# Layer 2 of a four-layer network: rows of B asked for earlier, tokens' transposes in the results' PSUM bank, expert-bias products moved into the send steps

## The chip, the core and the metric

The kernel runs on one core of one Trainium2 chip. The metric is the time of one execution on the device, in microseconds (us). Engines are named as in the profile: PE is TensorE, DVE is VectorE, ACT is ScalarE, POOL is GpSimd, and SP is SyncE, which issues most DMAs. Each engine works through its own instructions in the order in which they were issued and waits on semaphores for the others.

## The reference

The network has four layers on 16 sequences of 256 tokens with 128 features. Each layer normalises `x`, computes an attention-like part `s` and a feed-forward part `f` from the same normalised tokens, and adds `s * silu(f)` to `x`. The change lies in layer 2, whose two parts are these (shortened):

```python
# s: a selective scan (d_inner 256, 16 states per channel)
xi, z = split(layernorm(xn) @ W_in); xc = silu(conv4(xi) + conv_b)
dt_lo, B, C = split(xc @ W_xp, [8, 24]);  delta = softplus(dt_lo @ W_dt + dt_bias)
for t: h = h * exp(delta[t] * A) + (delta[t] * xc[t]) * B[t];  y[t] = (h * C[t]).sum(state)
s = ((y + xc * D_skip) * silu(z)) @ W_out + xn
# f: 16 experts (128 -> 512 -> 128), the two most likely of each token
p = softmax(xn @ Wr + br); gate = p at the two largest, 0 elsewhere
f = sum_e gate[:, e] * (relu(xn @ W1[e] + b1[e]) @ W2[e] + b2[e])
```

The part `gate @ b2` of `f` doesn't depend on the experts' results. It is computed by itself, as eight products of 128x512, and is what the text calls the bias products.

## The kernel before

All tokens stand in SBUF as 32 tiles of 128 tokens. `layer2` runs the scan of `attn2` and the experts of `ffn2` beside one another, in one long loop of steps written out in Python.

**The scan.** The 4096 tokens are eight groups of 512 (two sequences). A group takes 32 steps, so there are 256. Every even step handles two of the 16 states for one half of the 256 channels, for 512 tokens at once. DVE multiplies the input by the rows of B (`dbb`, L1113) and runs the scan (`st`, L1117). The product with the rows of C (`hc`, L1130) is made by POOL one pair of steps later, beside the next scan, or by DVE itself while POOL is sending tokens (steps below 32) and gathering them (from the step `fetch` on). ACT computes the decays (`dab`, L1103) four steps ahead. PE adds the products up over the states by multiplying with the identity (`sums`, L1140), five steps behind. There are two buffers for scans, three for `hc` and three for decays. `prepare` computes the inputs of the next group in small parts that are hung on steps; its products share the two PSUM banks `psa` (tile `pa`).

**Rows of B and C.** `broadcast(n)` asks SP for two rows of B and two rows of C from DRAM, each laid over 128 partitions (512 KB, L94). Both were asked for three steps ahead of their first use, and each kind has two buffers, so that a request waits until the last reader of its buffer is through.

**The experts.** The routing part of `ffn2` finds each token's two experts and its places in a DRAM buffer of 47 blocks of 256 rows (one expert for each block). Then:

- `send`: in steps 0 to 31 POOL writes the tokens to their places by 64 indirect DMAs, two per step (L1333).
- `begin`, in step 33, loads the tokens of the first blocks (L1345) and weights (L1354, L1356), and transposes two blocks.
- From step 34 on a `piece` per step, four to a block: PE multiplies by W1 (`hidden`, L1377, twice per block, into the bank `psh`), ACT applies bias and relu (`relu`, L1391), and PE multiplies the block before by W2 (`result`, L1402, two halves, into the bank `psy`). Beside the second half PE transposes the tokens of a later block (`turn`, L1365, into the bank `psh` too). One step later `evict` copies the result (L1414) and writes it to DRAM from SP (`store`, L1415), copies the transposed tokens (`turned`, L1370), and asks SP for the weights two blocks on and the tokens three blocks on.
- Two steps of every 32 hold no piece, so that `evict` falls on steps 2, 6, 10... of a cycle of four in one half of the time and on steps 0, 4, 8... in the other.
- `bring` and `weigh`, from step 239 on: POOL gathers each tile's two result rows (L1451, six buffers per kind) and DVE adds them to `f`, weighted (L1461); after every fourth tile come the gated addition and the normalisation for layer 3, whose `rstd` (L158, L159) is POOL's.

The routing ended with the bias products: PE multiplied (L1319) into the one PSUM buffer `tot`, ACT copied (L1320), eight times, before the buffer could be used again. The tile framework sets the order between this part and the first steps; within the loop of steps `pin` keeps each engine to the order in which the code was written.

```python
            for k in range(max(at) + 1):
                if k < SENT:
                    for i in range(2):
                        experts["send"](2 * k + i)
                scan["step"](k, k < SENT or k >= fetch)
                for f_ in at.get(k, ()):
                    f_()
```

Of the kernel before, what the change touches and what calls it, by code (L numbers as in the profile page):

```python
# [10 lines left out]
F32 = mybir.dt.float32  # L11
# [8 lines left out]
P = 128  # L20
# [53 lines left out]
class Net:  # L74
# [734 lines left out]
    def layer2(self, ydram, consts):  # L809
# [10 lines left out]
        with ExitStack() as ctx:  # L820
# [21 lines left out]


            k = SENT + 1
            later(k, experts["begin"])
# [75 lines left out]
    def attn2(self, ctx, psa, consts, later):  # L921
# [34 lines left out]
        def prepare(gr, base):  # L956
# [108 lines left out]

            def broadcast(n):
                for i, name in ((8, "bn"), (24, "cn")):
                    d[name, n] = self.load(
                        bc, d["dr"][i + n : i + n + 2, :].partition_broadcast(P), name, shape=[P, 2, T]
                    )  # L1070

# [9 lines left out]
            parts += [(25, delta), (26, inputs)]  # L1081
            parts += [(29 + 2 * n, call(broadcast, n)) for n in range(0, N, 2)]
            parts.sort(key=lambda p: p[0])
# [120 lines left out]
    def ffn2(self, ctx, consts, f):  # L1204
# [12 lines left out]
        gate = cp.tile([P, K, NT], F32, name="gate")  # L1217
        bank = cp.tile([P, NB], I32, name="bank")
        b1s = cp.tile([P, 4, NB], F32, name="b1s")
        with tc.tile_pool(name="f2_r", bufs=1, **side) as rp, tc.tile_pool(  # L1220
# [83 lines left out]
            for i in range(4):  # L1304
                nc.tensor.transpose(
                    pg[:, i, :], e[:, 8 * i : 8 * i + 8, :].rearrange("p t e -> p (t e)"), self.ident
                )
            gT = rp.tile([P, 4, P], F32, name="gT")
            nc.scalar.copy(gT, pg)


            b2 = rp.tile([P, 8, D], F32, name="b2")
            nc.gpsimd.memset(b2, 0.0)  # L1313
            for j in range(8):
                nc.sync.dma_start(b2[E * j : E * j + E, j, :], a["L2_ffn_b2"])
            for c in range(NT // 4):
                pf = ps.tile([P, 4, P], F32, name="tot")
                o = 4 * (c % 2)
                nc.tensor.matmul(pf, gT[:, c // 2, :], b2[:, o : o + 4, :], start=True, stop=True)  # L1319
                nc.scalar.copy(f[:, 4 * c : 4 * c + 4, :], pf)  # L1320

# [3 lines left out]
        rp = enter("f2_x", 3)  # L1325
        gp = enter("f2_g", 6)
        psh = enter("f2_ph", 1, space=PSUM)
        psy = enter("f2_py", 1, space=PSUM)
        placed, got = [], {}

        def send(i):
# [29 lines left out]
        def turn(j):  # L1361
            if j < NB:
                got[j]["px"] = px = psh.tile([P, R], F32, name="ph")
                for q in range(2):
                    nc.tensor.transpose(px[:, q * P : (q + 1) * P], got[j]["xr"][:, q, :], self.ident)  # L1365

        def turned(j):
            if j < NB:
                got[j]["xT"] = rp.tile([P, R], F32, name="xT")
                nc.scalar.copy(got[j]["xT"], got[j]["px"])  # L1370

# [23 lines left out]
        def result(j, q):  # L1395
            if j < 0:
                return
            if q == 0:
                got[j]["py"] = psy.tile([P, 2, D], F32, name="py")
            py, h, w2 = (got[j][n] for n in ("py", "h", "w2"))  # L1400
            for c in range(4):
                nc.tensor.matmul(  # L1402
                    py[:, q, :],
                    h[:, c, q * P : (q + 1) * P],
                    w2[:, c, :],
                    start=(c == 0),
                    stop=(c == 3),
                )

        def store(j):  # L1410
            if j < 0:
                return
            y = pool.tile([P, 2, D], F32, name="y")
            nc.scalar.copy(y, got.pop(j)["py"])  # L1414
            nc.sync.dma_start(ys[j * R : (j + 1) * R, :].rearrange("(q p) d -> p q d", p=P), y)  # L1415
# [43 lines left out]
        def weigh(t):  # L1459
# [7 lines left out]
            "send": send, "begin": begin, "piece": piece, "pieces": 4 * NB + 4, "bring": bring,  # L1467
            "weigh": weigh,
        }
# [494 lines left out]
```

## Time and profile before

| | us |
|---|---|
| median of three runs (lowest, highest) | 3040.19 (3035.48, 3047.49) |
| the profiled execution, its own time | 3071.67 |
| its span | 3069.7 |
| layer 2 from the first scan to the last (in the profile) | 875.2 to 1615.6 |

The page gives, for the whole span, PE as busy for 2502.2 us, DVE for 1997.0, ACT for 1479.0 and POOL for 1345.6. These are averages over very different stages; layer 2's loop of steps takes a quarter of the span, and what bounds it changes along the way. The lines of a timeline give start and duration in us, engine, line, operation, tiles and shape; in brackets stands the idle time of the engine before it and what ended that.

### The profile page before, as it was taken

The numbers are of one execution on the slowest core, as the hardware profiler recorded it, in microseconds if no ns is written. First come the engines' busy times: TensorE is split into PE (matmuls) and PEld (weight loads), VectorE is DVE, ScalarE is ACT, GpSimd is POOL, SyncE is SP. The second block draws the span as 40 slices with busy tenths as digits, with TensorE's granted clock in tenths as the row PEclk, the third lists the DMA queues.
The fourth block names the chain that finished last, engine by engine and source line by source line (L and its number), as shares of the span: only waits on it lengthen the run. The fifth ranks groups of instructions, "written<-read, shape, count | busy, mean of one in ns | idle before, by whom it ended". The sixth has DMA issues, their size and how long they took to land. (4 is left out here: it accounts for less than half of the span.)

```text
span 3069.7 us, 47743 instructions
## 1 busy us (share of the span) xinstructions
PE 2502.2 (82%) x17560; PEld 1605.9 (52%) x17575; DVE 1997.0 (65%) x4037; ACT 1479.0 (48%) x3291; POOL 1345.6 (44%) x1156
## 2 busy tenths in 40 slices
PE   5999893779654799999934688898999987899987
PEld 4666582556421455555513455554566654566654
DVE  5666433335573978787885467787778745788845
ACT  2555461223332566667621345443677641577743
POOL 2000002123327255555566788875455522455531
PEclk8999895879756799999966589898899989899988
DMA  2111002000112456555521211011000000000000
GB/s 66 29 29 29 4 2 98 1 18 14 39 55 85 139 174 195 169 185 183 176 94 41 46 25 39 22 37 51 13 13 14 15 1 2 14 15 15 13 3 28
DMA packets 136214, 168.24 MB, mean 55 GB/s; under 512 B 20658, under 2 KB 100413, under 8 KB 135981
## 3 DMA queue, kind: packets, MB, share of 16 engines
q1 hardware_dynamic: 127404, 147.09, 16.1%
q0 software_dynamic: 6496, 17.05, 1.6%
q8 instruction: 139, 2.28, 0.3%
q10 hardware_dynamic: 2080, 1.05, 0.1%
q14 instruction: 95, 0.77, 0.1%
HBM read 126.96 MB, written 29.79 MB: 51 GB/s over the span
## 5 line engine op out<-in xcount | busy, mean ns | idle before, releaser
L335 DVE TENSOR_REDUCE nmax<-pa 128x2 f32<-128x512 f32 x512 | 330.5, 684 | 151.2 <-PE pb L326 124.9
L316 PE MATMUL pa<-kT,qT 32*128 32x256 f32 x2048 | 388.0, 430 | 21.5 <-DMA kT<-qkd 10.8
L326 PE MATMUL pb<-qa,kT 32*128 32x256 f32 x2048 | 382.9, 418 | 6.9 <-ACT e L340 6.8
L340 ACT ACTIVATE e<-pb 128x512 f32<-128x512 f32 x512 | 280.2, 595 | 207.0 <-PE pb L326 204.9
L1130 POOL TENSOR_TENSOR hc<-st,cn 128x1024 f32<-128x1024 f32 x104 | 245.7, 2362 | 248.4 <-DVE dbb L1113 193.0
L316 PEld LDWEIGHTS pa<-kT,qT 32*128 32x128 f32 x2048 | 253.0, 199 | 120.9 <-issue 50.8
L1117 DVE TENSOR_TENSOR_SCAN st<-dab,dbb 128x1024 f32<-128x1024 f32 x128 | 292.7, 2287 | 25.3 <-POOL hc L1130 6.9
L1140 PE MATMUL py<-hc,ident 128*128 128x512 f32 x512 | 284.1, 653 | 23.6 <-POOL hc L1130 11.7
L326 PEld LDWEIGHTS pb<-qa,kT 32*128 32x128 f32 x2048 | 250.2, 193 | 20.5 <-ACT e L340 14.5
L343 POOL TENSOR_TENSOR e<-e,pen 128x512 f32<-128x512 f32 x176 | 234.3, 1356 | 42.1 <-ACT e L340 42.0
L1776 ACT ACTIVATE p<-ps,nm,rl 128x128 f32<-128x128 f32 x512 | 227.2, 464 | 42.3 <-DVE nm L1769 42.0
L1785 POOL TENSOR_TENSOR p<-p,den 128x512 f32<-128x512 f32 x128 | 132.8, 1038 | 246.1 <-DVE den L1784 224.8
L1103 ACT ACTIVATE dab<-dl,A_log 128x512 f32<-128x512 f32 x256 | 178.7, 717 | 115.9 <-DVE st L1117 73.8
L1687 PE MATMUL pm<-wqkv,hT 128*128 128x512 f32 x384 | 207.4, 654 | 17.8 <-DVE hT L1681 8.7
L1113 DVE TENSOR_TENSOR dbb<-du,bn 128x1024 f32<-128x1024 f32 x128 | 179.3, 1401 | 43.2 <-DMA bn<-dr 41.4
L1710 POOL TENSOR_TENSOR rot<-rot,sn 128x512 f32<-128x512 f32 x128 | 162.3, 1268 | 99.4 <-DVE sn L1705 83.1
L1140 PEld LDWEIGHTS py<-hc,ident 128*128 128x128 f32 x512 | 98.8, 209 | 114.8 <-issue 74.9
L1313 POOL MEMSET b<- 128x1024 f32 x1 | 1.0, 951 | 327.0 <-PE pm L367 327.0
L367 PE MATMUL pm<-e,vaug 128*32 128x256 f32 x2048 | 140.7, 420 | 0.5 <-POOL e L343 0.5
L1757 PE MATMUL ps<-kT,qT 64*64 64x128 f32 x2048 | 139.9, 289 | 0.0
L1757 PEld LDWEIGHTS ps<-kT,qT 64*64 64x64 f32 x2048 | 93.7, 137 | 82.0 <-issue 80.1
L1700 ACT ACTIVATE sq<-pm 128x512 f32<-128x512 f32 x128 | 74.9, 615 | 118.3 <-PE pm L1687 112.6
(372 smaller groups left out, 5556.5 us busy)
## 6 DMA issues: line engine op xcount, KB each, us to landing
bn<-dr SPq DMA_DIRECT2D x64, 512.0 KB
cn<-dr SPq DMA_DIRECT2D x64, 512.0 KB
w<-in_L_ffn_W_dram SPq DMA_DIRECT2D x94, 256.0 KB
qkd<-qk SPq DMA_DIRECT2D x32, 256.0 KB
v<-v SPq DMA_DIRECT2D x64, 128.0 KB
f_y<-y SPq DMA_DIRECT2D x47, 128.0 KB
f_x<-zero POOLq DMA_DIRECT2D x8, 704.0 KB
xr<-f_x SPq DMA_DIRECT2D x44, 128.0 KB
```

The lines of the kernel that those rows point to most:

```text
L316: nc.tensor.matmul(pa[:, t, :], qbuf[b % 4][r : r + 32, g, ts], kbuf[b % 4][r : r + 32, g, :], start=True, stop=True,)
L326: nc.tensor.matmul(pb[:, t, :], kbuf[b % 4][r : r + 32, g, ts], qas[m // 8][r : r + 32, g % 2, :], start=True, stop=True,)
L335: nc.vector.tensor_reduce(nbuf[n // 8 % 2][:, :, u // 4, u % 4, 8], pa, AX.X, ALU.max, negate=True)
L340: nc.scalar.activation(e, pb, AF.Exp, scale=scale)
L343: eng.tensor_mul(e, e, pens[m // 16])
L1113: mul = nc.vector.tensor_mul(db, du, d["bn", n])
L1117: nc.vector.tensor_tensor_scan(wide(d["st", r]), wide(d.pop(("da", r))), wide(db), 0.0, ALU.mult, ALU.add)
L1130: ins = eng.tensor_mul(d["hc", r], d.pop(("st", r)), d["cn", r // 4 * 2])
L1140: nc.tensor.matmul(d["py", h], self.ident, d["hc", r - r % 2][:, r % 2, :], start=(n == 0), stop=(n == N - 1))
L1687: nc.tensor.matmul(pj, hTs[b % 3][:, t * P : (t + 1) * P], d["qkv"][:, j * 512 : (j + 1) * 512], start=True, stop=True,)
L1757: nc.tensor.matmul(ps[i][64 * half : 64 * half + 64, c, w, :], qT[f, 2 * u + c, q0 : q0 + 64], kT[f, 2 * u + c, keys[half] : keys[half] + ...
L1776: nc.scalar.activation(p[:, c, w, :], ps[i][:, c, w, :], AF.Exp, scale=r[:, w, 0, h + 2 * c : h + 2 * c + 1], bias=nm[:, c, w : w + 1], ac ...
```

## The change

Four things are changed.

- The rows of B are asked for two steps earlier (position 27 + 2n in place of 29 + 2n); the rows of C stay.
- `turn` writes into the second half of the bank that holds the results; that bank is now one tile `halves` for the whole time, with `halves[:, 0]` for results and `halves[:, 1]` for transposed tokens.
- The bias products leave the routing. Step 1 clears a buffer (on DVE, before on POOL) and loads `b2` into it by eight small DMAs on SP; the eight products run in steps 4, 7, 16, 19, 22, 25, 28 and 31, each into a bank of `psa`, and ACT copies each one a step later.
- The gathers' buffers go from six to four per kind. The clearing buffer takes the place of one of the two buffers `h` until step 31.

```diff
@@ layer2
+            later(1, experts["spread"])
+            for c in range(NT // 4):
+                k = (4, 7, 16, 19, 22, 25, 28, 31)[c]
+                later(k, lambda c=c: experts["biases"](psa, c))
+                later(k + 1, lambda c=c: experts["biased"](c))
             k = SENT + 1
             later(k, experts["begin"])
@@ attn2, prepare
-            def broadcast(n):
-                for i, name in ((8, "bn"), (24, "cn")):
-                    d[name, n] = self.load(
-                        bc, d["dr"][i + n : i + n + 2, :].partition_broadcast(P), name, shape=[P, 2, T]
-                    )
+            def broadcast(name, n):
+                i = {"bn": 8, "cn": 24}[name] + n
+                d[name, n] = self.load(
+                    bc, d["dr"][i : i + 2, :].partition_broadcast(P), name, shape=[P, 2, T]
+                )
...
-            parts += [(29 + 2 * n, call(broadcast, n)) for n in range(0, N, 2)]
+            for n in range(0, N, 2):
+                parts += [(27 + 2 * n, call(broadcast, "bn", n)), (29 + 2 * n, call(broadcast, "cn", n))]
@@ ffn2, routing
+        gT = cp.tile([P, 4, P], F32, name="gT")
...
-            gT = rp.tile([P, 4, P], F32, name="gT")
             nc.scalar.copy(gT, pg)
-            b2 = rp.tile([P, 8, D], F32, name="b2")
-            nc.gpsimd.memset(b2, 0.0)
-            for j in range(8):
-                nc.sync.dma_start(b2[E * j : E * j + E, j, :], a["L2_ffn_b2"])
-            for c in range(NT // 4):
-                pf = ps.tile([P, 4, P], F32, name="tot")
-                o = 4 * (c % 2)
-                nc.tensor.matmul(pf, gT[:, c // 2, :], b2[:, o : o + 4, :], start=True, stop=True)
-                nc.scalar.copy(f[:, 4 * c : 4 * c + 4, :], pf)
...
-        gp = enter("f2_g", 6)
+        gp = enter("f2_g", 4)
...
         psy = enter("f2_py", 1, space=PSUM)
+        halves = psy.tile([P, 2, 2, D], F32, name="py")
+        def spread():
+            b2 = pool.tile([P, 4, R], F32, name="h")
+            got["b2"] = b2 = b2.rearrange("p c (o d) -> p (c o) d", d=D)
+            nc.vector.memset(b2, 0.0)
+            for j in range(8):
+                nc.sync.dma_start(b2[E * j : E * j + E, j, :], a["L2_ffn_b2"])
+        def biases(ps, c):
+            got["pf"] = pf = ps.tile([P, 4, P], F32, name="pa")
+            o = 4 * (c % 2)
+            nc.tensor.matmul(pf, gT[:, c // 2, :], got["b2"][:, o : o + 4, :], start=True, stop=True)
+        def biased(c):
+            nc.scalar.copy(f[:, 4 * c : 4 * c + 4, :], got["pf"])
@@ turn, turned, result, store
-                got[j]["px"] = px = psh.tile([P, R], F32, name="ph")
                 for q in range(2):
-                    nc.tensor.transpose(px[:, q * P : (q + 1) * P], got[j]["xr"][:, q, :], self.ident)
+                    nc.tensor.transpose(halves[:, 1, q, :], got[j]["xr"][:, q, :], self.ident)
...
-                nc.scalar.copy(got[j]["xT"], got[j]["px"])
+                nc.scalar.copy(got[j]["xT"], halves[:, 1].rearrange("p q d -> p (q d)"))
...
-            if q == 0:
-                got[j]["py"] = psy.tile([P, 2, D], F32, name="py")
-            py, h, w2 = (got[j][n] for n in ("py", "h", "w2"))
+            py, h, w2 = halves[:, 0], got[j]["h"], got[j]["w2"]
...
-            nc.scalar.copy(y, got.pop(j)["py"])
+            nc.scalar.copy(y, halves[:, 0])
+            del got[j]
```

More of the change, by code (lines that the diff above doesn't have):

```diff
@@ L1467, in ffn2 @@
             "send": send, "begin": begin, "piece": piece, "pieces": 4 * NB + 4, "bring": bring,
-            "weigh": weigh,
+            "weigh": weigh, "spread": spread, "biases": biases, "biased": biased,
         }
```

## The prediction

> **What bounds the kernel now.** I read three stages of layer 2 in the timeline, then the waits and PE's groups for steps 34 to 239.
>
> *Routing to sends.* The timeline around 911 to 937 us:
>
> ```profile
> 929.45 2.07 PE L1319 MATMUL tot<-b,gT 128*128 128x512 f32 x2 [0.68 <-ACT xnT L1320]
> 931.55 0.59 ACT L1320 COPY xnT<-tot 128x512 f32<-128x512 f32 x1 [2.16 <-PE tot L1319]
> 932.19 2.08 PE L1140 MATMUL py<-hc,ident 128*128 128x512 f32 x2 [0.68 <-ACT xnT L1320]
> ...
> 936.83 1.23 DVE L1130 TENSOR_TENSOR hc<-st,cn 128x1024 f32<-128x1024 f32 x1 [25.86 <-PE py L1140]
> ```
>
> Product and copy alternate on one buffer, 2.75 us for each of eight (910.2 to 932.2). The sums stand behind them on PE, no `hc` buffer comes free, and DVE stands for 25.86 us. Later in the same timeline:
>
> ```profile
> 972.69 1.34 PE L1014 MATMUL pa<-xz,W_xp 128*40 128x512 f32 x2
> 992.75 0.96 POOL L1333 DMA_INDIRECT f_x<-xn,slot  x1 [0.30 <-issue]
> 995.52 2.25 POOL L1345 DMA_DIRECT2D xr<-f_x  x3 [1.81 <-DMA f_x<-xn,slot]
> 1000.04 0.58 ACT L1020 COPY xd<-pa 40x512 f32<-40x512 f32 x1 [19.68 <-remote]
> 1000.09 1.22 DVE L1130 TENSOR_TENSOR hc<-st,cn 128x1024 f32<-128x1024 f32 x1 [9.98 <-remote]
> ```
>
> ACT copies a product that PE had finished at 974.03 only at 1000.04: between about 945 and 1000, while POOL sends, PE's signals come late. DVE waits 8.00, 10.67, 5.74 and 9.98 us before four `hc`: 34.4 us. POOL's sends run from 911.3 at 1.26 us each whatever the others do, and the first tokens can be loaded from 995.5.
>
> *Expert pieces.* The waits from 1040 to 1548, two of PE's groups there, and two windows in which DVE stands:
>
> ```profile
> DVE dbb L1113 <- DMA bn<-dr: 41.4, 19, 7.5
> POOL hc L1130 <- PE py L1140: 39.6, 17, 5.7
> ...
> L1377 PE MATMUL ph<-xT,w 128*128 128x256 f32 x376 | 103.0, 398 | 18.4 <-ACT xT L1370 18.1
> L1365 PE MATMUL ph<-ident,xr 128*128 128x128 f32 x90 | 18.3, 285 | 18.4 <-ACT h L1391 18.3
> ...
> 1150.00:1155.00 5.00, 5.00 (x20) 2.50 (x18) 0.00 (x0) 4.94 (x5) 0.00 (x0) 1.00 0.90 231
> 1308.00:1314.00 6.00, 6.00 (x23) 2.98 (x21) 0.00 (x0) 5.94 (x6) 0.64 (x1) 1.00 0.88 250
> ```
>
> In the windows (length, then busy time and count of PE, PEld, DVE, ACT, POOL) DVE does nothing, waiting for rows of B, and PE is busy all along; so it is in every such wait that I opened. PE's idle time is 41 of these 508 us, and 36.4 of that is the bank which `turn` shares with `hidden`. PE sets the pace here; the rows are late because they stand on SP behind a `store` that waits for PE.
>
> *Gathers.*
>
> ```profile
> 1636.84 1.30 DVE L172 TENSOR_SCALAR xn<-x,ln_mv,ln_r 128x128 f32<-128x128 f32 x4 [4.40 <-POOL ln_r L159]
> 1636.99 1.13 POOL L1451 DMA_INDIRECT got<-f_y,slot  x1 [0.19 <-issue]
> 1637.87 1.38 DVE L1461 SCALAR_TENSOR_TENSOR xnT<-got,gate,xnT 128x128 f32<-128x128 f32 x4
> ```
>
> From 1612 to 1656 POOL never stands for more than 0.5 us and DVE waits for it.
>
> **The change, part by part.** The sum is made against the profiled execution, 3071.67 us, and then carried to the median, which is 31.5 us lower.
>
> *Bias products out of the routing.* Sums can follow the copy of `gT` at 910.2, so `hc` runs at about 911 in place of 936.8: 25.8 us sooner for the scan. What is late next is the tokens. Undisturbed, six pairs of steps and a `prepare` took 1002.6 to 1037.9, that is 5.1 us a pair and 4.9 extra. Before without late signals: scan of step 8 at 939.3, of step 32 at 939.3 + 12 x 5.1 + 4.9 = 1005.4. After: at 980. But `turn` in step 33 needs tokens that land at about 1000, and PE holds the sums behind it; so the first expert product starts at about 1003 in place of 1007 (1040.4 in the profile, with the 34.4 us). With late signals in both, it moves from 1040.4 to about 1017, or to 1003 if they vanish. The gain in this stage is therefore 3 to 4 us at the least and 23 to 37 at the most. Which end counts is decided by whether runs without a profile have late signals. The profiled execution is 31.5 us above the median, close to the 34.4; I take them for the profile's own and count 4 us.
>
> *Bias products in the steps.* Eight products (2 x 0.43 to 1.04 us), eight copies of 0.59 on ACT, on engines that are busy for 49 and 19 of the 100 us from 900 on. In steps 8 and 19 a `prepare` product must wait for the copy to free a bank; behind that wait on PE are sums which DVE needs a pair later. All of it ends before the tokens come: nothing, or at most 8 x 0.59 + 2 x 5.1 = 15 us if DVE, not the tokens, were last. The clearing on DVE lies before the places are known, where DVE is busy for 33 of 36 us: 1 us (POOL took 0.95 for the same shape). Eight DMAs at 0.32 to 0.42 on SP's queue in step 1 stand ahead of the rows for step 8 on: 3 us there, against rows due some 12 us later, so none.
>
> *`turn` in the results' bank.* `turn` no longer waits for `relu`, `hidden` no longer for the copy of the tokens. Not all returns. The next `hidden` needs the same `relu`, after 0.3 us of transposes and 0.86 of sums; the next `result` needs the copy `y`, which stands just ahead of `xT` on ACT. The gaps in PE's timeline: three of 3.64 us, where `hidden` and a sum (1.7) certainly fit, and after which the clock is down (`hidden` 2.08 for 1.03, sum 1.91 for 1.02, `result` 1.92 for 1.05: 2.8 us more); six of 1.68 to 3.18 on `relu`, of which 1.2 each; three of 1.28, gone. Least: 3 x 1.7 + 6 x 1.2 = 12. Most: 36.4 + 3 x 2.8 = 45. I take 3 x 4.5 + 6 x 1.2 + 3 x 1.28 = 25, since the gaps lie where ACT is late for its own reasons. A cost: `y` waits for the transposes (0.2 us), the next `result` for the copy `xT` (0.38). Between stand a sum, `hidden` and a sum, 2.6 us at full clock, which hide it.
>
> The Trainium skill ("PSUM — Partial Sum Buffer", section on bank collisions) speaks against this part: PSUM is to be guarded by whole bank, so that two halves of one bank can't be written by PE and read by ACT at once. If nothing hid that, 47 blocks by 0.6 us would take back 28 us, and the sum would end near the median of before.
>
> *Rows of B.* Where `evict` falls on steps 2, 6, 10, the order on SP stays what it was, as nothing stands between the old and the new place. Where it falls on 0, 4, 8, and at the change-over, the rows now pass one `store`, two weights and one load of tokens, and that is where the long waits are (before steps 60, 64, 80, 124, 144, 188, 208). Passed over, these wait at most for a product that DVE has made. The waits of 41.4 us go, but PE was busy through them: 0 to 41, and I count 0 on top of the 25, which DVE could not follow without it.
>
> *Four gather buffers.* `bring(t)` must now wait for `weigh(t-4)`. Laid over the trace, 13 of 32 tiles were issued up to 4.9 us ahead of that, 30.7 us together. Most lie where POOL had time in hand; in the stretch from 1612 three (tiles 22, 26, 30) come straight after POOL's `rstd`, 1.6 us each. Between 0 and 31; I take 5.
>
> Sum: 4 + 25 - 1 - 5 = 23 less. Unprofiled 3040.2 - 23 = **3017 us**; a profile would show about 20 to 30 us more off, some 3020 of its own time.
>
> **The rivals.**
>
> 1. *Late signals are real.* Then the 23 to 37 us of the first stage count, taken as 31: 3040 - 31 - 25 + 6 = 2990. For: they hold ACT and DVE alike. Against: the 31.5 us.
> 2. *The pace is DVE's.* The rows' 41.4 come whole, in place of the 25: 3040 - 4 - 41 + 6 = 3001. Against: PE full in the windows.
> 3. *The stalls only move.* PE's waits reappear at `result` and at ACT, 6 us stay: 3040 - 4 - 6 + 6 = 3036, no change. For: ACT is busy for 339 of 508 us and in order.
> 4. *Slower: the gathers.* POOL and DVE take turns. From 31 us, if each measured wait is passed on, to 8 x 7.4 = 59 if DVE's work per four tiles (2.8 weighing, 1.4 adding, 1.9 statistics, 1.3 normalising) never overlaps POOL's 10: middle 45, 3040 - 4 - 25 + 1 + 45 = 3057. It decides from 43 us on, or 31 with only 12 from PE.
>
> **How the numbers follow.** About 0.5% (15 us) is what a measurement of this kernel can tell from no change: faster ends at 3025, slower begins at 3055. Chances: forecast 0.45, rivals 0.22, 0.05, 0.15, 0.13. The forecast's own range is 3003 to 3031; a quarter of it is above 3025. Faster: 0.34 + 0.22 + 0.05, and 0.02 of the third; slower 0.13, of the fourth and the worst of the third; the same 0.24. The range 2984 to 3050 leaves out the lower third of the first rival and most of the fourth.
>
> **What would show it.** L1140 follows L1305 on PE, and DVE's 25.86 us go. L1365 has no wait for L1391, L1377 at most a few us for L1370; `dbb` waits for `bn` under 8 us; PE's idle time from the first to the last piece falls from 41 to under 20 us, and those pieces take some 483 us in place of 508. POOL shows waits for L1461 in the gathers. Wrong if the first expert product starts as late as before, if PE's waits return under L1402, or if the stretch from the first gather to the last is longer by over 10 us.

## The result, and the profile after

The changed kernel takes 3039.16 us (median of 12 runs, 3034.81 to 3052.78); the kernel before, on the same chip, 3044.29 us (12 runs). The ratio is 0.9983 with a 95% interval of 0.9964 to 1.0002: 5 us less, and by this measurement no change. Its profiled execution took 3041.83 us, with a span of 3039.9. So 27 of the 30 us between the two profiled executions are the excess of the one of before over its own median (3071.67 against 3044.29).

In the changed kernel the lines have moved: `dbb` L1119, `st` L1123, `hc` L1136, sums L1146, send L1347, tokens L1359, `turn` L1378, `turned` L1383, `hidden` L1390, `relu` L1404, `result` L1413, `y` L1425, gathers L1463, `weigh` L1473; in `prepare`, `rest` is L1053, `exact` L1061, `delta` L1064, and POOL's last writes to `dl` are L1069.

The timeline of the changed kernel from the first send on (start, duration, engine, line; in brackets the idle time before):

```profile
901.52 3.03 POOL L1347 DMA_INDIRECT f_x<-xn,slot  x1 [44.37 <-DVE slot L1279]
...
906.04 1.23 DVE L1136 TENSOR_TENSOR hc<-st,cn 128x1024 f32<-128x1024 f32 x1
...
916.90 1.22 DVE L1119 TENSOR_TENSOR dbb<-du,bn 128x1024 f32<-128x1024 f32 x1
916.99 1.96 POOL L1347 DMA_INDIRECT f_x<-xn,slot  x1 [0.30 <-issue]
```

No `hc` stands for 25.86 us any more; from there until 985 us DVE never stands for more than 0.5 us. But the send that begins at 916.99, while DVE is in `dbb`, takes 1.96 us, where most take 0.96. At the end of the sends:

```profile
985.49 2.29 DVE L1123 TENSOR_TENSOR_SCAN st<-dab,dbb 128x1024 f32<-128x1024 f32 x1
...
999.50 2.25 POOL L1359 DMA_DIRECT2D xr<-f_x  x3 [1.91 <-issue]
...
1002.11 0.69 PE L1378 MATMUL py<-ident,xr 128*128 128x128 f32 x2 [25.26 <-DMA xr<-f_x]
...
1006.30 1.90 PE L1390 MATMUL ph<-xT,w 128*128 128x256 f32 x4
...
1006.54 0.75 DVE L1152 SCALAR_TENSOR_TENSOR xz<-xz,D_skip,py 128x512 f32<-128x512 f32 x1 [18.76 <-PE py L1146]
```

The scan reaches the step that needs the tokens 20 us early, and PE and DVE stand until they land. The 25.86 us have become 25.26 on PE and 18.76 on DVE.

For the expert pieces, the waits from 1007 to 1511 (engine, tile and line, what ended the wait: total us, times, longest):

```profile
ACT dab L1109 <- POOL dl L1069: 30.5, 6, 6.1
DVE du L1053 <- ACT u L1050: 28.0, 6, 5.5
...
PE py L1413 <- ACT xT L1383: 12.3, 6, 2.8
...
PE py L1378 <- DMA xr<-f_x: 11.3, 12, 2.2
...
PE ph L1390 <- ACT h L1404: 8.7, 6, 2.4
...
DVE dbb L1119 <- DMA bn<-dr: 3.0, 6, 1.1
```

DVE's 41.4 us for rows of B are 3.0, and PE's 36.4 us between `turn` and `hidden` on the shared bank are gone. In their place DVE waits for `u` 28.0 us (17.4 before), and PE waits at `result` for the copy `xT`, at `turn` for the tokens, and at `hidden` itself for `relu`. PE's idle time from step 36 to 240 is 39.5 us (40.8 before). One of the windows in which DVE now stands, ahead of a `rest`:

```profile
1131.60:1136.80 5.20, 5.20 (x27) 3.66 (x26) 0.00 (x0) 4.97 (x9) 1.78 (x1) 1.00 0.32 96
```

It looks like those of before (DVE nothing, PE full), but the thing waited for is another. In the gathers, from 1510 to 1627:

```profile
POOL got L1463 <- DVE xnT L1473: 18.7, 12, 3.1
```

`bring` waits for `weigh`, as foreseen, and first to last gather takes 115.1 us.

### The profile page after: what moved, and what is told of

Its sections match the earlier page's. It is cut to its first block, busy times and chain, and to the rows that moved or that the text cites. A ratio compares the mean times of both kernels' runs of the same rounds, so it can differ in the third digit from the quotient of the medians.

```text
span 3039.9 us, 47776 instructions
## 1 busy us (share of the span) xinstructions
PE 2481.5 (82%) x17560; PEld 1603.5 (53%) x17575; DVE 2015.2 (66%) x4038; ACT 1475.7 (49%) x3291; POOL 1361.3 (45%) x1155
## 5 line engine op out<-in xcount | busy, mean ns | idle before, releaser
L1136 POOL TENSOR_TENSOR hc<-st,cn 128x1024 f32<-128x1024 f32 x104 | 247.0, 2375 | 203.2 <-DVE dbb L1119 105.1
L1123 DVE TENSOR_TENSOR_SCAN st<-dab,dbb 128x1024 f32<-128x1024 f32 x128 | 292.8, 2287 | 31.5 <-POOL hc L1136 11.2
L1146 PE MATMUL py<-hc,ident 128*128 128x512 f32 x512 | 277.7, 639 | 21.5 <-POOL hc L1136 13.9
L1699 PE MATMUL pm<-wqkv,hT 128*128 128x512 f32 x384 | 204.0, 644 | 18.2 <-DVE hT L1693 8.7
L158 POOL TENSOR_SCALAR ln_r<-ln_mv 128x4 f32<-128x4 f32 x32 | 7.5, 233 | 471.0 <-DVE ln_st L168 418.0
L1119 DVE TENSOR_TENSOR dbb<-du,bn 128x1024 f32<-128x1024 f32 x128 | 195.1, 1524 | 5.3 <-DMA bn<-dr 3.0
L1146 PEld LDWEIGHTS py<-hc,ident 128*128 128x128 f32 x512 | 96.8, 205 | 108.9 <-issue 83.0
L1413 PEld LDWEIGHTS py<-w,h 128*128 128x128 f32 x752 | 100.1, 195 | 60.6 <-issue 37.7
```

Of the source, the lines that this page charges most:

```text
L1119: mul = nc.vector.tensor_mul(db, du, d["bn", n])
L1123: nc.vector.tensor_tensor_scan(wide(d["st", r]), wide(d.pop(("da", r))), wide(db), 0.0, ALU.mult, ALU.add)
L1136: ins = eng.tensor_mul(d["hc", r], d.pop(("st", r)), d["cn", r // 4 * 2])
L1146: nc.tensor.matmul(d["py", h], self.ident, d["hc", r - r % 2][:, r % 2, :], start=(n == 0), stop=(n == N - 1))
L1699: nc.tensor.matmul(pj, hTs[b % 3][:, t * P : (t + 1) * P], d["qkv"][:, j * 512 : (j + 1) * 512], start=True, stop=True,)
```

## The experiments

The starts of the scan's steps mark the same points in every kernel. The table has, from each profile, the first expert product counted from the first scan, the time from the scan of step 36 to that of step 240 (the pieces), and first to last gather; and the ratio of the times to those of before, with its interval.

| run | ratio | first product | 36 to 240 | gathers |
|---|---|---|---|---|
| before | 1 | 165.2 | 500.4 | 107.9 |
| changed kernel | 0.9983 (0.9964 to 1.0002) | 130.4 | 501.2 | 115.1 |
| rows_alone | 0.9987 (0.9969 to 1.0004) | 137.3 | 501.8 | 107.1 |
| turn_alone | 0.9984 (0.9970 to 0.9998) | 134.3 | 502.4 | 106.4 |
| bias_alone | 0.9989 (0.9973 to 1.0006) | 127.9 | 502.4 | 115.0 |
| gathers4_alone | 1.0023 (1.0012 to 1.0034) | 138.6 | 505.6 | 115.4 |
| pe_light | 0.9924 (0.9895 to 0.9953) | 127.6 | 482.3 | 114.6 |
| dve_light | 0.9999 (0.9977 to 1.0022) | 130.3 | 504.2 | 114.6 |
| prep_early | 0.9964 (0.9938 to 0.9990) | 127.8 | 494.2 | 115.4 |
| turn_early | 0.9998 (0.9972 to 1.0024) | 128.3 | 502.9 | 115.1 |
| sends_one_operand | one run | 126.2 | 501.5 | 114.8 |
| pieces_one_operand | 0.9954 (0.9933 to 0.9975) | 127.4 | 490.8 | 115.0 |
| scan_further_ahead | 0.9951 (0.9934 to 0.9968) | 134.4 | 501.1 | 116.0 |
| prep_dve_gather6 | 0.9910 (0.9895 to 0.9926) | 128.4 | 481.9 | 106.3 |
| all_of_these | 0.9876 (0.9857 to 0.9894) | 131.4 | 479.9 | 109.1 |
| all_but_turn | 0.9880 (0.9857 to 0.9902) | 133.6 | 479.7 | 109.2 |
| all_but_rows | 0.9905 (0.9884 to 0.9925) | 133.4 | 485.1 | 109.2 |
| all_turn_sooner | 0.9945 (0.9908 to 0.9982) | 131.6 | 506.8 | 109.1 |
| all_pe_light | 0.9825 (0.9797 to 0.9854) | 131.6 | 461.7 | 109.1 |

Each stage is from one profile. before and gathers4_alone, whose pieces are the same, differ by 5.2 us in them, so that a difference of that size in the pieces alone is no finding.

### The parts of the change, one at a time

**rows_alone**, against the kernel before:

```diff
-            parts += [(29 + 2 * n, call(broadcast, n)) for n in range(0, N, 2)]
+                parts += [(27 + 2 * n, call(broadcast, "bn", n)), (29 + 2 * n, call(broadcast, "cn", n))]
```

> The kernel before, with rows of B asked for two half-steps sooner and nothing else changed. Theory 'stalls move': DVE's 41.4 us of waits for bn go to under 8 us, but dbb then starts earlier and meets POOL's hc and the waits of the prepare chain (du for u, dl for u) grow by as much; time within 5 us of before. Rival 'a part eats the gain of another' : rows are worth 10 us or more by themselves (faster by over 0.3%), or cost as much because tokens now land behind them.

501.8 us, and a time that can't be told from before.

**turn_alone**: `halves`, with `turn`, `turned`, `result` and `store` as in the change.

> The kernel before, with the tokens' transposes in the results' bank and nothing else changed. Theory 'stalls move': PE's 36.4 us of waits on the bank of hidden go, but come back at result (for the copies y and xT) and at the tokens, the pieces take 508 us as before; time within 5 us of before. Rival 'eaten by another part': this part alone gives the 12 to 25 us of the prediction, and one of the other parts takes it back.

502.4 us. The ratio is worth 5 us with an interval of 1 to 9, which the pieces of the profile do not show; 12 to 25 is out of the question.

**bias_alone**: `spread`, `biases` and `biased` in the send steps, `gT` kept, four gather buffers.

> The kernel before, with the bias products in the send steps, gT kept, and four gather buffers in place of six (without that it doesn't fit); rows of B and the transposes as before. Theory 'stalls move': the 25.86 us before the second hc go, sends begin 10 us sooner but each takes 1.5 us in place of 1.26 while DVE is busy, so the tokens land some 3 to 10 us later than the scan needs them and the first expert product starts 5 to 10 us sooner at most; the gathers take 7 us more; together within 6 us of before. Rival 'eaten': this part is slower than before by 7 us or more by itself, so that it hides a gain of the transposes.

The first expert product comes 127.9 us after the first scan. In rows_alone, turn_alone and gathers4_alone, whose send stage is that of before, it comes after 137.3, 134.3 and 138.6; so this part is worth some 9 us, and the gathers take most of it back.

**gathers4_alone**:

```diff
-        gp = enter("f2_g", 6)
+        gp = enter("f2_g", 4)
```

> The kernel before with four gather buffers in place of six and nothing else changed. Theory: bring waits for weigh of four tiles before; the stretch from first to last gather grows by some 7 us (107.9 to 115 us) and so does the time (+4 to +9 us). Rival: the 7 us seen there in the changed kernel come from the earlier start, and this alone costs 0 to 2 us.

7 us slower (0.0023 x 3040; interval 4 to 10), and the gathers show it. POOL's waits there:

```profile
POOL got L1451 <- DVE xnT L1461: 19.9, 15, 3.4
```

So no part hides another's large gain: "eaten" falls, and the pieces are 500 to 506 us with each part and without.

### What paces the pieces

**pe_light**, against the changed kernel:

```diff
-            for c in range(4):
+            for c in range(2):
...
-                    stop=(c == 3),
+                    stop=(c == 1),
```

> The changed kernel with half of the second expert product left out (two of four products in each result): 376 products of 0.112 us less on PE, 42 us, between steps 36 and 240, which take 501 us in every profile so far; the other engines keep their work. Theory A (PE sets the pace of the pieces, 437 us of products at the spacing of the full clock, 40 us idle and the rest a lower clock): 36 to 240 falls by 35 to 45 us. Theory B (DVE sets it: 420 us busy and some 50 us of waits in the prepare chain, in order): it falls by 0 to 8 us. Theory C (a ring: PE, ACT and DVE take turns in holding each other up): 12 to 28 us.

18.9 us of the 42 arrive, so PE sets the pace for a part of the time only. That is theory C's range, not A's.

**dve_light**:

```diff
+            if h == 1 and self.SENT + 8 <= k < self.fetch:
+                outputs(k - 2, False)
+                db = d["bn", n]
+            else:
...
```

> The changed kernel with the product of du and B left out in every second pair of the pieces (the scan reads the rows of B as they are): some 50 dbb of 1.6 us less on DVE, 75 to 80 us, and as many less that can collide with POOL's hc. Theory A (PE sets the pace): steps 36 to 240 stay at 501 us within 8. Theory B (DVE): they fall by 50 to 78 us, until PE's 460 binds, so at least 40. Theory C (a ring): 12 to 28 us.

504.2 us, but the run doesn't answer its question. DVE's groups between steps 36 and 240 (busy us, mean ns of one, then the idle time before them and what ended it):

```profile
L1127 DVE TENSOR_TENSOR_SCAN st<-dab,bn 128x1024 f32<-128x1024 f32 x50 | 130.3, 2606 | 23.0 <-ACT dab L1109 19.8 <-POOL hc L1140 0.2
L1127 DVE TENSOR_TENSOR_SCAN st<-dab,dbb 128x1024 f32<-128x1024 f32 x53 | 121.2, 2287 | 24.5 <-POOL hc L1140 18.3 <-DVE dbb L1123 0.5
L1123 DVE TENSOR_TENSOR dbb<-du,bn 128x1024 f32<-128x1024 f32 x52 | 119.2, 2291 | 5.8 <-DMA bn<-dr 5.7
```

A scan that reads `bn` from SBUF takes 2606 ns in place of 2287, and the `dbb` that are left 2291 in place of 1598: DVE's busy time fell by 18 us (421.7 to 403.6), not by 75. DVE's weight had to be asked in another way. (The expectation of all_but_rows, below, still counts these 80 us as left out; 18 were.)

**pieces_one_operand**:

```diff
+            if self.SENT <= k < self.fetch:
+                mul = nc.vector.tensor_scalar_mul(flat(db), flat(d["bn", n]), 0.5)
...
```

> The changed kernel with dbb in the steps of the pieces made from B alone (half of B in place of du times B): DVE reads one operand from SBUF there. In the changed kernel 102 of these products take 162.9 us, 1598 ns each, where one undisturbed takes 1.22; so 38 us of DVE's time go, and nothing is added elsewhere. Theory B (DVE sets the pace): steps 36 to 240, 501.2 us, fall by 25 to 38 us. Theory A or D (PE and the prepare chain set it, DVE has time in hand): 0 to 6 us, and DVE waits longer for u, dl or bn.

DVE's group of `dbb` there:

```profile
L1121 DVE TENSOR_SCALAR dbb<-bn 128x1024 f32<-128x1024 f32 x101 | 123.8, 1225 | 8.5 <-DMA bn<-dr 6.3
```

39 us of DVE's time went, and 10.4 us of the pieces: above the range of A and D, far below B's. POOL's products beside it became shorter as well (its busy time fell from 300.3 to 285.3 us), so DVE's weight isn't seen by itself. Most of what is gained lies in steps 28 to 31 of a group, as the table below and prep_dve_gather6 show.

**prep_early**:

```diff
-            parts += [(14, silu), (16, call(down, 0)), (17, call(down, 1)), (18, downed)]
-            parts += [(19, call(up, 0)), (19, call(up, 1)), (20, call(biased, 0)), (20, call(biased, 1))]
-            parts += [(21, size), (21, small), (22, plus), (23, rest), (23, log), (24, exact)]
+            parts += [(14, silu), (16, call(down, 0)), (16, call(down, 1)), (17, downed)]
+            parts += [(18, call(up, 0)), (18, call(up, 1)), (19, call(biased, 0)), (19, call(biased, 1))]
+            parts += [(20, size), (20, small), (20, plus), (22, rest), (22, log), (23, exact)]
```

> The changed kernel with the tail of each prepare (the products W_xp and W_dt, the bias, Abs, Exp and the 1 + u) asked for one or two steps sooner, and rest, log and exact one step sooner, so that a step more lies between ACT's or POOL's part and DVE's. Nothing is left out. In the changed kernel DVE waits 28 us for ACT's u and 14.9 for POOL's u in six prepares, and ACT waits 30.5 us for POOL's dl, behind which the copies y and xT stand that PE's result needs. Theory A (PE's throughput): 501 us stay within 5. Theory D (the prepare chain stops ACT and DVE six times, and PE behind them): the waits fall to a third and 36 to 240 falls by 12 to 30 us. Theory C (a ring): DVE's and ACT's waits fall, but others take their place, 0 to 8 us less.

The waits of this run from step 36 to 240:

```profile
ACT dab L1109 <- POOL dl L1069: 26.0, 6, 4.8
...
DVE du L1053 <- ACT u L1050: 5.3, 6, 1.6
```

DVE's wait for `u` fell from 28.0 to 5.3, ACT's for POOL's `dl` hardly, and 7 us came out: below D's range, and within C's. What ACT waits for had not been touched.

**turn_early**:

```diff
-                return lambda: result(j - 1, 0), lambda: None
+                return lambda: (result(j - 1, 0), turn(j + 2)), lambda: turned(j + 2)
...
+                tokens(j + 3, nc.sync)
                 store(j - 1)
-                turned(j + 2)
                 weights(j + 2)
-                tokens(j + 3, nc.sync)
```

> The changed kernel with the tokens' transposes and their copy in the half step after the first half of result, where ACT has nothing from the pieces, in place of the step of store, and the load of tokens ahead of store on SP. Nothing is left out. PE's waits for the copy xT (12.3 us, at result) and for the tokens (11.3 us) should go. Theory A (PE sets the pace): 36 to 240 falls by 15 to 24 us. Theories B, C and D (others hold PE up in any case): 0 to 6 us less, and PE's idle time turns up at other lines, 30 us or more in all.

502.9 us with 44.7 us of idle time on PE. PE's waits from step 36 to 240:

```profile
PE py L1413 <- ACT xT L1383: 16.1, 6, 3.2
...
PE py L1378 <- DMA xr<-f_x: 12.0, 6, 2.8
```

The two waits that should go are still there (12.3 and 11.3 us in the changed kernel): `result` stands behind the copy `xT` as before, now with its second half. So this run took nothing away, and doesn't tell A from the others.

**Where in the group.** `prepare` repeats every 32 steps, so the pieces can be laid over one another: mean length in us of each stretch of four steps, from scan to scan, over the five groups of steps 64 to 223, worked out from the traces; DVE's busy time is the sum of its durations. (gathers4_alone stands for before; in this stretch the two are alike.)

```
steps of the group   0-3   4-7   8-11  12-15  16-19  20-23  24-27  28-31   sum
gathers4_alone       8.00  9.43  9.13  12.46   8.62  11.05  12.06   9.27  80.0
rows_alone           7.94  9.37  9.04  10.05   9.21  13.79  11.00   9.48  79.9
turn_alone           8.19  9.70  8.46  12.58   8.69  10.03  11.98   9.52  79.1
changed kernel       7.94  9.47  8.91  10.05   9.50  13.24  10.94   9.49  79.5
  its DVE busy       7.76  9.04  7.72   8.25   8.14   8.31   8.27   9.15  66.6
  its PE idle        1.13  0.18  0     0       0.21   0.06   2.43   2.15   6.2
pe_light             8.35  9.37  8.09   9.16   8.97  12.14  10.93   9.48  76.5
pieces_one_operand   8.50  8.18 10.61   9.17  10.19  13.44  10.91   7.36  78.4
prep_early           8.57  9.37  9.10  10.06   9.55   9.81  12.48   9.49  78.4
prep_dve_gather6     7.89  9.37  8.20   9.98   9.41  14.16   9.72   7.43  76.1
```

One group has several limits. In steps 0 to 7 and 28 to 31 DVE's busy time nearly fills the stretch (9.04 of 9.47, 9.15 of 9.49), and pieces_one_operand shortens 4 to 7 and 28 to 31; 8 to 11 take back what 4 to 7 gave. In steps 8 to 23, with `prepare`'s products, PE has hardly a gap while DVE has several; pe_light gains there. From 24 on PE is ahead and idles, and `prepare`'s tail on DVE, POOL and ACT seems to set the time; that is read from the table alone. PE's waits on the bank lay in steps 16 to 31: of the 6.6 us per group for which PE idles in the profile of before, 4.7 are in steps 24 to 31, and hardly any in 4 to 15. Of DVE's 41.4 us of waits for rows, half (20.8 us, 4.2 per group) lay in steps 12 to 15 and a third in 24 to 31. In 12 to 15 rows_alone gains 2.4 us, and it gives 2.7 back in steps 20 to 23, where DVE comes to wait for `u`, whose products are at the end of PE's full stretch.

### The sends

**sends_one_operand**, with `dbb` of the steps below 32 as in pieces_one_operand:

> The changed kernel with dbb in the 16 pairs of the send steps made from B alone (half of B in place of du times B), so that DVE reads one operand from SBUF there and not two; the products of C stay. In the changed kernel 63 sends take 95.1 us where 63 x 1.264 would be 79.6; some 14 of them are longer by 1.0 us, each begun while DVE was in a product of two SBUF operands. Theory P (DVE and POOL take turns at a port whenever DVE reads two operands from SBUF): the collisions with dbb go, those with hc stay, the sends take 82 to 90 us, the first expert product starts 5 to 13 us before 1006 us of the span. Rival (the descriptors' queue slows the sends, whatever DVE reads): 93 to 97 us, and the first expert product at 1004 to 1008.

The sends take 88.5 us, against 95.1 in the changed kernel and 92.9 to 95.1 in the other profiles with this send stage: theory P. The first expert product starts at 998.4 us of the span, 7.9 sooner; counted from the first scan it is 126.2 against 127.4 to 130.4 in the other profiles with this send stage, so 1 to 4 us of it are sure, less than theory P had. The first send takes 1.08 us in place of 3.03, though DVE's clearing (L1336 here) stands beside it as before: what had held it up was the `dbb` behind the clearing. From the timelines of DVE and of POOL (start, duration):

```profile
915.73 1.22 DVE L1121 TENSOR_SCALAR dbb<-bn 128x1024 f32<-128x1024 f32 x1
```

```profile
915.82 0.96 POOL L1351 DMA_INDIRECT f_x<-xn,slot  x1 [0.31 <-issue]
...
919.61 1.88 POOL L1351 DMA_INDIRECT f_x<-xn,slot  x1 [0.30 <-issue]
```

A send begun 0.09 us into this `dbb` is no longer held up (the one at 916.99 above was). The one at 919.61 is: it begins 0.18 us into an `hc`, which still reads two operands.

**scan_further_ahead**:

```diff
-            SENT, STEPS = self.SENT, 256
+            SENT, STEPS = 40, 256
...
-                if k < SENT:
+                if k < 32:
                     for i in range(2):
```

> The changed kernel with the pieces begun at step 41 in place of 33, and the 64 sends in the first 32 steps as before; nothing is left out. In the changed kernel the scan stands from 985.5 to 1008.6 us, since the step that needs the tokens is reached 20 us before they land. Theory T (the tokens' landing sets the start of the pieces, whatever the scan does): the first expert product starts at 1006 within 4 us, the pieces take 504 us within 5, and eight steps of the scan fewer lie in the gathers, which take 100 to 110 us in place of 115; 5 to 15 us less in all. Rival (the gathers' length is that of POOL and the four buffers): gathers 113 to 117 us, within 5 us of the changed kernel.

Start and pieces are as theory T has them (1012.6 us of the span, a little beyond its 4; first product to first gather 500.4 us), but the gathers don't shorten: there the rival is right. Still the kernel is 15 us faster than before. Layer 3's first step comes 28.2 us after the last gather in place of 37.6. The last scan now begins 100 us before the last gather (1529.0 and 1629.1), not 46 (1579.9 and 1625.9), so the scan's last outputs can be done sooner; neither theory had this, and it was not tried apart.

### Versions that follow

**prep_dve_gather6**: prep_early, and

```diff
-            eng = nc.vector if busy else nc.gpsimd
+            eng = nc.vector
...
-        rp = enter("f2_x", 3)
-        gp = enter("f2_g", 4)
+        rp = enter("f2_x", 2)
+        gp = enter("f2_g", 6)
...
```

(With two buffers `begin` loads two blocks of tokens from POOL, and the third from SP.)

> The changed kernel with the prepare's tail sooner (as in the run prep_early), its last products on DVE in place of POOL (exact, inputs and the markers), and six gather buffers paid for by two buffers in place of three for the tokens and their transposes; nothing is left out. Theory D (the prepare chain over POOL stops ACT and DVE): ACT's wait for POOL's dl (26.0 us in prep_early) and DVE's for u go, steps 36 to 240 fall from 494.2 to 480 to 490 us; the gathers fall from 115 to 107; 3010 to 3022 us in all. Theory C (a ring in which other waits take their place): 36 to 240 stays at 494 within 4, gathers 107: 3020 to 3030 us.

ACT's longest wait for `prepare`, again from step 36 to 240:

```profile
ACT dab L1109 <- DVE dl L1069: 12.3, 6, 2.8
```

ACT's wait at the decays halves (26.0 to 12.3), and 494.2 becomes 481.9, in theory D's range, now by 19 us against the changed kernel. Gathers 106.3 us. 27 us faster than before.

But the time doesn't go where theory D has it. From prep_early to this run the stretches of steps 28 to 31 fall from 56.9 to 44.5 us in all, 12.4 us; the rest of the pieces, taken together, stays at 437. In steps 28 to 31 of the changed kernel each group has one `dbb` like this (from the timelines of DVE and POOL):

```profile
1152.53 3.34 DVE L1119 TENSOR_TENSOR dbb<-du,bn 128x1024 f32<-128x1024 f32 x1
```

```profile
1152.43 2.35 POOL L1136 TENSOR_TENSOR hc<-st,cn 128x1024 f32<-128x1024 f32 x1
```

It begins 0.1 us after an `hc` of POOL and takes 2.1 us more than the 1.23 of others; six of them make 12.7 us. With POOL's last products on DVE that meeting is gone, and the mean `dbb` there is 1.26 us. pieces_one_operand, which leaves POOL's products where they were, gains as much in these steps (56.9 to 44.2). So the end of this meeting is worth the gain by itself; that the shorter wait of ACT gave any of it is not shown.

**all_of_these**: this with scan_further_ahead.

> The run before this with the pieces begun at step 41 as well; nothing is left out. Theories D and T: the gains add, 3000 to 3015 us. Theory C or the rival on the gathers: within 5 us of the better of the two runs before.

2997.81 us, a ratio of 0.9876 (0.9857 to 0.9894): 38 us faster than before, and the fastest complete version here, a little below the range of D and T: the gains add.

**all_but_turn**: `turn` back in the bank `ph`, the rest as in all_of_these.

> The run all_of_these (2997.81 us, steps 36 to 240 in 479.9) with the tokens' transposes back in the bank that hidden uses; nothing is left out. Theory M (the prepare chain masked the gain): 36 to 240 grows by 10 to 25 us, 3008 to 3023 us. Theory N (PE's waits on that bank cost nothing in themselves; what holds PE is ACT, which comes late with relu and with the copies alike): it grows by 0 to 5 us, 2996 to 3003 us.

479.7 us against 479.9, with a ratio of 0.9880 against 0.9876 (another chip, where before took 3038.69 us). Theory N. Two of PE's groups from 993 to 1475, first of all_of_these, then of all_but_turn:

```profile
L1390 PE MATMUL ph<-xT,w 128*128 128x256 f32 x372 | 98.9, 389 | 14.4 <-ACT h L1404 14.4
...
L1378 PE MATMUL py<-ident,xr 128*128 128x128 f32 x94 | 18.8, 282 | 11.5 <-DMA xr<-f_x 11.0 <-ACT xT L1383 0.5
```

```profile
L1390 PE MATMUL ph<-xT,w 128*128 128x256 f32 x372 | 99.1, 389 | 12.0 <-ACT h L1404 6.1 <-ACT xT L1383 5.7
...
L1378 PE MATMUL ph<-ident,xr 128*128 128x128 f32 x94 | 18.8, 282 | 11.9 <-ACT h L1404 10.3 <-DMA xr<-f_x 0.7 <-ACT dab L1109 0.5
```

25.9 us of waits with the new bank, 23.9 with the old: the same sum under other names.

**all_but_rows**: rows of B as before, the rest as in all_of_these.

> The run all_of_these with the rows of B asked for as before, two half-steps later; nothing is left out. Theory M: DVE's waits for bn return (30 to 45 us) and, with the prepare chain no longer in the way, cost 10 us or more. Theory N (DVE has time in hand: leaving out 80 us of its products changed nothing): they return and cost 0 to 5 us.

DVE's longest waits from step 36 to 240 are for the rows again:

```profile
DVE dbb L1118 <- DMA bn<-dr: 33.2, 18, 6.7
```

33.2 us of waits return and cost 5.2 in the pieces: at the upper edge of N, and no more than the pieces of two profiles can differ by. The ratios, 0.9905 against 0.9876, would make it 9, but their intervals overlap.

**all_turn_sooner**: turn_early on all_of_these.

> The run all_of_these with the transposes and their copy in the half step after the first half of result and the tokens loaded ahead of store, as in the run turn_early; nothing is left out. Theory M: PE's waits for xT and tokens were masked too, 36 to 240 falls by 8 to 15 us. Theory N: within 4 us of 479.9, with PE's idle time at relu instead.

Both theories missed: 506.8 us, 27 longer. ACT's longest wait, and one of its 42 cases (the transposes, the next `hidden`, the copy):

```profile
ACT xT L1383 <- PE ph L1390: 106.9, 42, 4.8
```

```profile
1152.29 0.38 PE L1378 MATMUL py<-ident,xr 128*128 128x128 f32 x2
...
1154.22 1.03 PE L1390 MATMUL ph<-xT,w 128*128 128x256 f32 x4
...
1155.29 0.37 ACT L1383 COPY xT<-py 128x256 f32<-128x256 f32 x1 [2.95 <-PE ph L1390]
```

The copy doesn't wait for the transposes, which end at 1152.67, but for `hidden`, which ends at 1155.25. In all_of_these `xT` has two buffers, so the copy for block j + 2 goes into the buffer of block j, and with the copy moved forward the second `hidden` of block j has yet to read it. ACT works in order, and decays and `relu` stand behind the copy. In turn_early, with three buffers, the copy waits for the transposes (30.0 us in all). So this run shows the price of the missing buffer, and leaves open whether PE's waits for `xT` and the tokens were masked; three buffers were not tried here.

**all_pe_light**: pe_light on all_of_these.

> The run all_of_these with half of the second expert product left out, as in pe_light (42 us of PE's products less). There it took 19 us off 501.2 us. Theory D (PE paces the steps in which prepare's products lie, the prepare chain the others): with that chain shortened PE paces more of the group, and 36 to 240 falls from 479.9 by 22 to 40 us. Theory C (a ring in which each engine weighs a part): 10 to 20 us, as before.

18.2 us of 42, as in pe_light (18.9). PE did not come to pace more once the tail was shorter: theory C, and a limit to theory D.

## Why the prediction was right or wrong

The forecast of 3017 us failed; its third rival, "the stalls only move" (3036), came out, at 0.15. Its waits under `result` are there; that its time fits to 3 us owes something to luck, since of its terms (4 and 6 us gained, 6 lost) none was measured at that size.

*`turn` in the results' bank, 25 us: the step that failed.* Measured: nothing in the pieces (500.4 against 501.2, and 479.7 against 479.9 in the better version). The reasoning behind "12 at the least" took PE's gaps to be time that the end waits for, because "PE sets the pace here". That had been read from windows in which DVE waits for rows, and through these waits PE is indeed busy, all 41.4 us; the two windows that the prediction shows lie in steps 12 to 15 of a group. It was then used for other moments, PE's gaps in steps 16 to 31, of which nothing had been read but that PE stands. In pe_light 42 us less of PE's products gave 18.9, so PE sets the pace for a part of the time only. That the gaps cost nothing is shown by turn_alone and all_but_turn; that they do so because PE is ahead of the others there is read from the table, and not shown by a run of its own. What the prediction said would show it wrong did show: PE's waits under `result` (12.3 us), and with them those for the tokens' DMA (11.3) and at `hidden` for `relu` (8.7), which it had not counted. PE's idle time stayed at 39 us where under 20 was expected, and the pieces at 501.

*The rule on PSUM banks* (the Trainium skill, "PSUM — Partial Sum Buffer", section on bank collisions) was to cost up to 28 us. Neither end is seen: both layouts take the same time. Since `result` is put off until `xT` is copied, none of the 92 copies `y` and `xT` between steps 36 and 240 of the changed kernel's profile overlaps with a product or a transpose in that bank, so the runs say nothing of a collision's price.

*Rows of B, 0 us.* Right: 501.8 us in rows_alone, and 5 us (9 by the ratios) in the better version. The reason given holds: in the profile of before PE idles for 0.0 of these 41.4 us. `u` is what DVE meets next.

*Bias products and the send stage, 4 us.* 7.6 us by the profiles: the mean of 130.4 and 127.9 against that of 137.3, 134.3 and 138.6. The mechanism (the tokens' landing is next) was right, and the choice to take the late signals for the one profiled execution's own was right too: in the other profiles step 8 to 32 of the scan takes 63 to 65 us, there 98.6. Mis-sized was the landing. "Sends run at 1.26 us whatever the others do" was read where DVE stood still for 34 us, and even there one send that met a `dbb` took 1.96 us:

```profile
942.98 1.96 POOL L1333 DMA_INDIRECT f_x<-xn,slot  x1 [0.30 <-issue]
```

With DVE at work the 63 spacings take 89.7 us in gathers4_alone and 95.1 in the changed kernel, where that profile has 81.5.

*The four gather buffers, 5 us.* 7 (4 to 10), and 8.0 in the profiles (the mean of 115.1, 115.0 and 115.4 against that of 107.9, 107.1 and 106.4). *Clearing on DVE, 1 us*: 0.91 (L1332); it is part of the 7.6 above.

*The other rivals.* Real late signals (2990) and the whole 41.4 us of the rows (3001) are refuted by rows and stages above; the gathers' slow case (45 us) too, since POOL waited 18.7 us for `weigh` and the stretch grew by 7.

With the measured terms the sum is 7.6 + 0 - 8.0, about 0, and the median came out 5 us lower with an interval from 11 lower to 1 higher.

## What to carry to other kernels

Where work repeats with a period, lay the periods over one another and ask for each part of it which engine is full there; a stall is worth its removal only in the part where its engine is the one that all others wait for. Before a wait is removed, name the next thing that the same engine needs and when that is ready: DVE's 41 us for rows of B became waits for `u`, and PE's 36 us on a bank became waits for a copy, a load and `relu`. When something is moved forward, ask who still reads the buffer that it writes (all_turn_sooner). The largest gain here, 19 us in the pieces, came from `prepare`'s tail over ACT, DVE and POOL: 7 us from asking for it sooner, and 12 where one product of DVE per group no longer met one of POOL, which no list of waits shows, since a held-up product counts as busy.

## What the runs showed of the hardware

- **DVE and POOL hold each other up when DVE reads two operands from SBUF.** Of the sends in the changed kernel, thirteen that begin 0.04 to 0.11 us into such a product of DVE (1.22 us) take 1.0 us longer, and the first, which meets a `dbb` on its way, 2.1; six that begin 0.02 or 0.03 us into one are not held up. Scans, with one operand in PSUM, hold up none of the 18 sends that begin in them, nor does `dbb` from one operand any of 15 in sends_one_operand. Together that is 95.1 - 63 x 1.264 = 15.5 us. In the pieces `dbb` takes 1598 ns in the mean in place of 1225 with one operand, and one that begins just after an `hc` of POOL 3.34 us. The Trainium skill ("SBUF — State Buffer", section "Who interferes with whom") states the rule, that a DVE instruction with two SBUF inputs contends with a GpSimd instruction that reads SBUF; these runs agree and show that sends with places read from SBUF are among those. The same section infers that `tensor_tensor` doesn't stall DMAs that GpSimd issues; twelve of the thirteen sends above were held up by one, and the measurement decides.
- **Layer 3, untouched by any of these kernels, took 1364.6 to 1376.7 us** in the profiles, from its first step to the end. A difference of under 12 us between two single profiles' spans is no finding; the stage's own stretch is.
